# Row sums of exp(a) in a two-layer graph kernel: by a row of ones, or by partition

## The chip, the cores and the metric

The kernel runs on one core of a Trainium2 chip. Times are device microseconds of that core, and the metric is the median of several runs. Everything is in fp32; each fp32 matmul of the program appears in the profile as two TensorE instructions.

## The reference

The input is `x` (3327 x 512) and a sparse, symmetric-pattern adjacency `adj` (3327 x 3327). Two layers follow one another.

```
h = relu(layernorm(x))
a = (h Wq^T + bq)(h Wk^T + bk)^T / sqrt(512) + adj + adj
x = x + softmax(a, axis=-1) (h Wv^T + bv)

h = relu(layernorm(x))
A2 = adj + I
dscale = diagonal(A2) ** -0.5
x = x + relu((dscale[:,None] * A2 * dscale[None,:]) @ (A2 @ h @ W^T))
```

The softmax has a denominator for each row of `a`: the sum of exp(a) over 3327 entries. The change concerns these sums alone.

## The kernel before

Rows are padded to 3328, which is 26 tiles of 128. The kernel has three parts: it makes h^T and the queries, then the scores and their exponentials, then three large products (with exp(a), and twice with `adj`), each a one-level seven-multiplication scheme over 2 x 2 blocks.

**The scores.** The transposed scores are made in four groups, one for each entry (s, q) of `groups = [(1, 0), (0, 0), (0, 1), (1, 1)]`. Strip s has 2 x 7 tiles of 128 columns (s = 0) or 2 x 6 (s = 1); a group takes a half q of it, so its width `wd` is 448 columns (s = 0) or 384 (s = 1), for both halves y of the strip. Within a group the loop runs over 13 pairs of row tiles (`HALF = 13`). A step is one pair: `Pair.multiply` issues seven products of two program matmuls each (28 TensorE instructions) into banks of PSUM called X, Y and Z, and after each product VectorE adds it into the tile `g` (lines 557 and 565). ScalarE takes the exponentials (560 and 567). The work of neighbouring steps is put between the products by a hand-written list of seven entries, `beside_of(k)`, whose entry runs after a given product. In this loop VectorE, TensorE, GpSimd and SyncE keep the order of the program (`in_order`); ScalarE does not, and at the border to the next stage, which has an order of its own, the build interleaves the two.

**What accumulates.** The rows of a step lie on the partitions, so summing over rows of the transposed scores means summing over partitions and over the 13 steps. `Pair.gather` adds, step by step, two combinations of the exponentials into the tile `acc` (128 x 2 x wd): `acc[:, 0]` holds the sum of S1 terms and `acc[:, 1]` that of S4 terms, as the seven-multiplication scheme has made them. The sums of the strip's second half are those of `acc[:, 0]`; those of its first half are `acc[:, 1]` minus `acc[:, 0]`. It runs at two steps' distance: the last pair of a group is gathered in the second step of the next group.

**What turns it into sums.** `Pair.total(m)`, lines 601 to 613, runs once per group and m, two entries apart in the same step. It multiplies a column of ones (the stationary operand, 128 x 1) with `acc[:, m]` (the moving one, 384 or 448 columns), so that one row of sums lands on partition 0 of PSUM. VectorE copies that row (609) or subtracts the earlier one from it (611), and SyncE stores it to `totd` in DRAM (613). The last group is dealt with in the second step of the graph stage by `totals()`, which gives both sums the same bank, `ROLE["p8"]`; the others take turns in banks 6 and 7 (`tp_bank`).

**What reads it.** Two steps later `load_totals` (674) loads `totd` back as `tot`, 128 x 26, so that the sum of a row stands on the partition of that row. `prepared` takes the reciprocal (740), `judge` (691 to 703) tests the range of the sums, and `attend` (1016) scales rows with the reciprocal, some 400 us later.

**The graph stage.** `Step.multiply` (912) takes the seven products of one step, 14 instructions of 384 or 448 columns; its left operands, tiles `part`, are loaded three steps ahead by SyncE and summed by VectorE (175 to 177), its right operands `b` are loaded as `rows` and `row` (852) and combined (182 to 185, 873). A list `between` gives the step in which each further task runs.

Elsewhere in the kernel, line 463 multiplies a stationary 128 x 128 tile with the column of ones, four times in a row, for the bias of the queries; and 305 is a warm-up of TensorE at the start on a tile `zero`, which VectorE fills after three smaller memsets.

Of the kernel before, what the change touches and what calls it, by code (L numbers as in the profile page):

```python
# [10 lines left out]
F32 = mybir.dt.float32  # L11
# [4 lines left out]
P = 128  # L16
# [19 lines left out]
HALF = 13  # L36
PAIRS = 6
STRIPS = (0, 14)
HT = (7, 6)
# [8 lines left out]
def graph_layers_kernel(  # L48
# [29 lines left out]
    nc = tc.nc  # L78
    N = out.shape[0]
    NP, D = x.shape  # L80
# [29 lines left out]
    def bank(k, name):  # L110
        return banks.tile([P, BW], F32, name=name, tag=f"bank{k}")
# [27 lines left out]
    const = ctx.enter_context(tc.tile_pool(name="const", bufs=1))  # L139
    dram = ctx.enter_context(tc.tile_pool(name="dram", bufs=1, space=bass.MemoryType.DRAM))  # L140
# [5 lines left out]
    nc.vector.memset(mhalf, -0.5)  # L146
    ones = const.tile([P, 1], F32, name="ones")
    nc.vector.memset(ones, 1.0)

    pad = const.tile([P, 1], F32, name="pad")  # L150
    nc.vector.memset(pad, 0.0)
# [6 lines left out]
    tot = const.tile([P, NT], F32, name="tot")  # L158
# [5 lines left out]
    qd = dram.tile([P, DC, NP], F32, name="qd")  # L164
    pd = [[dram.tile([P, len(E_AT), H[s]], F32, name=f"p{s}_{t}") for t in range(HALF)] for s in range(2)]
    sumd = [[dram.tile([P, len(SUMS), H[s]], F32, name=f"sum{s}_{t}") for t in range(HALF)] for s in range(2)]
    totd = dram.tile([1, NP], F32, name="totd")
    x1d = [dram.tile([P, D], F32, name=f"x1d{i}") for i in range(NT)]
    rowd = [[dram.tile([P, D], F32, name=f"row{g}_{i}") for i in range(NT)] for g in range(3)]
    normd = {k: [dram.tile([1, 2 * 4 * P], F32, name=f"norm{m}_{k}") for m in range(2)] for k in range(4)}  # L170
# [56 lines left out]
    def psum_ring(*ks):  # L227
        turn = itertools.cycle(ks)
        return lambda name: bank(next(turn), name)

    x_bank, y_bank, z_bank, tp_bank = psum_ring(0, 1), psum_ring(2, 3), psum_ring(4, 5), psum_ring(6, 7)
# [203 lines left out]
    ps = [bank(k, "mm") for k in range(DC)]  # L435
    begun = h_transposed(TURN[0], psum_ring(6, 7, 4, 5))
    weighed = half(12, [P, D], "weighed")
    for c in range(DC):
# [8 lines left out]
        for r in range(DC):  # L447
            nc.tensor.matmul(ps[r], w_q[c // 2][:, c % 2, r * P : (r + 1) * P], w_k[c // 2][:, c % 2],
                             start=c == 0, stop=c == DC - 1)
# [60 lines left out]
    def adjacency(s, q, t):  # L510
# [6 lines left out]
            nc.sync.dma_start(g[k], src[:, :, c : c + wd])  # L517
        return g

    class Pair:  # L520


# [68 lines left out]
        def gather(self, m):  # L591

            if self.t == 0 and m == 0:
                Pair.acc = acc_ring([P, 2, Q[0]], "acc")[:, :, : self.wd]
            acc, new = Pair.acc, self.last if m else self.g[0][:, 1]
            if self.t == 0:
                nc.scalar.copy(acc[:, m], new)
            else:
                nc.vector.tensor_add(acc[:, m], acc[:, m], new)

        def total(self, m, own=None):

            if self.t < HALF - 1:
                return
            acc, ps = Pair.acc, own or tp_bank("tot")
            nc.tensor.matmul(ps[:1, : self.wd], ones, acc[:, m], start=True, stop=True)
            row = acc[:1, m]
            if m == 0:
                nc.vector.tensor_copy(row, ps[:1, : self.wd])
            else:  # L610
                nc.vector.tensor_sub(row, ps[:1, : self.wd], acc[:1, 0])
            c0 = (STRIPS[self.s] + (1 - m) * HT[self.s]) * P + self.c
            nc.sync.dma_start(totd[:, c0 : c0 + self.wd], row)


    pairs = {}
# [7 lines left out]
    def beside_of(k):  # L624
        def on(j, what, *args):
            if 0 <= j < len(steps):
                getattr(pairs[j], what)(*args)

        def difference():
            if k < len(steps) and steps[k][1] >= 6:  # L630
                next(more_of, None)

        return (
            lambda: (on(k - 2, "s4"), on(k - 2, "gather", 0)),
            lambda: (on(k - 1, "s3"), on(k - 2, "gather", 1)),
            lambda: on(k + 1, "sum_of_adjacency", 0),
            lambda: on(k + 1, "sum_of_adjacency", 1),
            lambda: (on(k - 2, "total", 0), difference()),
            lambda: (on(k - 2, "total", 1), on(k - 1, "s1")),
            lambda: on(k - 1, "s2"),  # L640
        )

    coming = queries(0)
# [7 lines left out]
    with in_order(*(e.engine for e in (nc.vector, nc.tensor, nc.gpsimd, nc.sync))):  # L651
        for k, (n, t) in enumerate(steps):
            if t == 0:
                qt = coming
            fetch(k + 2)
            if t == 2 and n + 1 < len(groups):
                coming = queries(n + 1)
                more_of = more_queries(n + 1, coming)
            beside = beside_of(k)
            pairs[k].multiply(qt)  # L660
        k = len(steps)
        beside = beside_of(k)
        for what in beside[:2]:
            what()
        Chain.finish()
        for what in (*beside[5:], *beside_of(k + 1)[:2]):
            what()

    def totals():
        for m in range(2):  # L670
            pairs[len(steps_of_scores) - 1].total(m, bank(ROLE["p8"], "tot"))

    def load_totals():
        nc.sync.dma_start(tot, totd[0].rearrange("(i p) -> p i", p=P))

    steps_of_scores = steps

# [2 lines left out]
    ROLE = {"p1": 0, "p6": 2, "p7": 4, "p5": 6, "p2": 7, "p3": 1, "p4": 5, "p8": 3}  # L680
# [79 lines left out]
    def difference():  # L760
        next(differences[0])
# [359 lines left out]
    def number_of(g, r, s, t):  # L1121
        return ((g * len(ORDER) + r) * 2 + s) * len(every) + t

    def at(k, what, *args):
        between.setdefault(k, []).append((what, args))

    early = []
    for g in range(3):
        for n, r in enumerate(ORDER):
            for t, e in enumerate(every):  # L1130
                k = number_of(g, n, 0, t)
# [9 lines left out]
    for n, job in enumerate(jobs):  # L1141
        k = k0 + n * (k1 - k0) // len(jobs)
# [15 lines left out]
    k = number_of(0, 5, 1, 2)  # L1158
# [6 lines left out]
    k = number_of(1, 5, 1, 2)  # L1165
# [9 lines left out]
    for (n, s, t), its in {  # L1175
# [4 lines left out]
        for i, when in zip(its, (between, within)):  # L1180
            if i is not None:
                k = number_of(2, n, s, t)
# [3 lines left out]
        rows(2, number_of(2, 4, 0, t + 2), i, (1,))  # L1186
    for n, i in enumerate(range(20, NT, 2)):
        at(number_of(2, 6, 1, 2) + n, last_load, i)
    for k, what in ((1, totals), (3, load_totals), (2, prepare), (6, prepared), (8, judge), (9, judged)):
        at(k, what)  # L1190
    k = number_of(1, 4, 0, 0)
    at(k, other_weights)
# [480 lines left out]
```

## Time and profile before

| | us |
|---|---|
| median of 3 runs | 2176.13 |
| lowest and highest run | 2174.09, 2177.01 |
| span of the profiled execution, first to last instruction | 2173.6 |
| the profiled execution's own time beside its span | not listed; the runs lie 0.5 to 3.4 above the span |
| TensorE busy | 2155.3 (99%) |
| VectorE busy | 1671.8 (77%) |
| ScalarE busy | 236.3 (11%) |
| DMA queues, share of 16 engines | 70.5% and 8.7% |
| the 16 instructions of line 606 | 244.2 to 639.1 us from the start, 511 ns by the median |
| the 8 VectorE instructions of lines 609 and 611 | 245.1 to 639.6 us, 576 ns by the median |

In the profile PE is TensorE's matmul row and PEld its weight loads, which can run beside a matmul. DVE is VectorE, ACT ScalarE, POOL GpSimd and SP SyncE, which only issues DMAs here. A timeline row gives the start in us, the length in us, the engine, the line, the operation, what is written and read, the shape of the stationary operand (for TensorE) and of the data, and the count of instructions merged into it; in brackets stands the idle time ahead of it, and what ended that. Lengths of matmuls overlap, because an instruction's end includes a modelled tail; starts are the better measure of pace. The mean granted TensorE clock is 0.999 of full speed.

### The profile page before, as it was taken

How to read it: one execution, taken by the hardware profiler on the slowest of the kernel's cores; microseconds unless marked ns; L12 is line 12 of the kernel's file. 1: busy time of each engine (PE TensorE's matmuls, PEld its weight loads, DVE VectorE, ACT ScalarE, POOL GpSimd, SP SyncE). 2: the span in 40 equal slices, each digit the busy share in tenths (PEclk: the TensorE clock that was granted, in tenths of full speed). 3: DMA queues.
4: the chain of work that ended last, by engine and by line, in shares of the span. 5: the costliest groups of instructions: out<-in, count | busy, mean ns of one | idle time of the engine just before them, and what ended most of it. 6: DMA issues, size and time to landing. Idle time of an engine off the chain costs nothing.

```text
span 2173.6 us, 21026 instructions
## 1 busy us (share of the span) xinstructions
PE 2155.3 (99%) x6378; PEld 1189.6 (55%) x6378; DVE 1671.8 (77%) x3256; ACT 236.3 (11%) x359; POOL 50.8 (2%) x62
## 2 busy tenths in 40 slices
PE   9999999999999999999999999999999999999998
PEld 5555555455555555555454555555666655555555
DVE  7479888888877688877778777987676667778686
ACT  6312111112110000000001000000011100000011
POOL 2000000000000000000111000000000000000000
PEclk9999999999999999999999999999999999999999
DMA  8678888889989899889787889986646468766695
GB/s 303 208 257 300 302 302 277 303 283 312 310 282 316 293 371 327 278 295 309 265 311 260 303 285 357 313 307 212 215 136 204 142 199 276 254 190 211 217 304 194
DMA packets 302030, 586.04 MB, mean 270 GB/s; under 512 B 34626, under 2 KB 169684, under 8 KB 301908
## 3 DMA queue, kind: packets, MB, share of 16 engines
q1 hardware_dynamic: 266614, 515.12, 70.5%
q10 hardware_dynamic: 35294, 69.48, 8.7%
q8 instruction: 53, 0.87, 0.2%
q14 instruction: 69, 0.57, 0.1%
HBM read 416.64 MB, written 167.86 MB: 269 GB/s over the span
## 4 chain that ended last, share of the span: by engine, by line
PE 91%; DVE 4%; DMA 4%; issue 1%; SPq 0%; POOL 0%; ACT 0%; ACTq 0%; DVEq 0%
PE p L912 52%; PE Y L553 13%; PE Z L553 7%; PE p L904 5%; PE p L1004 4%; PE pw L1065 3%; PE X L553 3%; PE Y L409 2%; DMA rows<-row 1%; PE Z L409 1%; DMA xt<-in_x_dram 1%; DVE part L175 1%; DMA part<-sum 1%; PE pt L1094 1%; PE X L409 0%
## 5 line engine op out<-in xcount | busy, mean ns | idle before, releaser
L912 PE MATMUL p<-part,b 128*128 128x448 f32 (+1 forms) x3528 | 1261.7, 513 | 2.2 <-DVE part L176 1.3
L912 PEld LDWEIGHTS p<-part,b 128*128 128x128 f32 x3528 | 668.0, 190 | 537.0 <-issue 286.1
L553 PE MATMUL Y<-qt,hp 128*128 128x448 f32 (+1 forms) x832 | 308.4, 513 | 1.7 <-DVE g L565 1.7
L175 DVE TENSOR_TENSOR part<-part 128x896 f32<-128x896 f32 (+1 forms) x252 | 256.8, 1019 | 67.3 <-DMA part<-sum 29.1
L553 PEld LDWEIGHTS Y<-qt,hp 128*128 128x128 f32 x832 | 157.7, 190 | 136.0 <-issue 72.3
L553 PE MATMUL Z<-qt,hp 128*128 128x384 f32 (+1 forms) x416 | 162.6, 513 | 0.0
L177 DVE TENSOR_TENSOR part<-part,part 128x448 f32<-128x448 f32 (+1 forms) x219 | 129.4, 591 | 14.9
L176 DVE TENSOR_TENSOR part<-part,part 128x448 f32<-128x448 f32 (+1 forms) x219 | 129.4, 591 | 7.2
L904 PE MATMUL p<-part,b 128*128 128x448 f32 (+1 forms) x336 | 124.2, 513 | 0.0
L553 PEld LDWEIGHTS Z<-qt,hp 128*128 128x128 f32 x416 | 78.8, 190 | 67.4 <-issue 37.4
L557 DVE SCALAR_TENSOR_TENSOR g<-g,Y 128x384 f32<-128x384 f32 (+1 forms) x156 | 91.4, 586 | 31.4 <-PE Y L553 30.3
L904 PEld LDWEIGHTS p<-part,b 128*128 128x128 f32 x336 | 63.7, 190 | 53.5 <-issue 31.4
L940 ACT COPY part<-p 128x384 f32<-128x384 f32 (+1 forms) x33 | 16.6, 502 | 660.2 <-PE p L912 543.2
L553 PE MATMUL X<-qt,hp 128*128 128x384 f32 (+1 forms) x208 | 81.1, 513 | 0.0
L560 ACT ACTIVATE g<-g 128x768 f32<-128x768 f32 (+1 forms) x48 | 43.0, 896 | 348.4 <-DVE g L557 298.7
L1004 PE MATMUL p<-w,ct 128*128 128x512 f32 x136 | 61.8, 594 | 0.4 <-DVE part L1016 0.4
L941 DVE TENSOR_TENSOR part<-p,part 128x384 f32<-128x384 f32 (+1 forms) x33 | 19.3, 585 | 52.9 <-PE p L912 52.2
L553 PEld LDWEIGHTS X<-qt,hp 128*128 128x128 f32 x208 | 39.5, 190 | 33.1 <-issue 19.3
L1065 PE MATMUL pw<-w,rows 128*128 128x256 f32 x208 | 53.6, 380 | 0.8 <-DVE rows L1055 0.8
L995 DVE TENSOR_TENSOR job<-job 128x896 f32<-128x896 f32 (+1 forms) x52 | 52.9, 1017 | 0.0
L202 POOL TENSOR_TENSOR rstd<-ve,mhalf 128x1 f32<-128x1 f32 x46 | 38.0, 828 | 555.4 <-DVE ve L200 520.9
L565 DVE TENSOR_TENSOR g<-g,Z 128x384 f32<-128x384 f32 (+1 forms) x52 | 30.4, 585 | 26.5 <-PE Z L553 26.4
(196 smaller groups left out, 1692.9 us busy)
## 6 DMA issues: line engine op xcount, KB each, us to landing
part<-sum SPq DMA_DIRECT2D x104, 448.0 KB, 5.3
part<-p SPq DMA_DIRECT2D x91, 448.0 KB, 6.0
part<-sum SPq DMA_DIRECT2D x104, 384.0 KB, 3.5
part<-p SPq DMA_DIRECT2D x91, 384.0 KB, 4.7
part<-in_adjT_dram SPq DMA_DIRECT2D x78, 448.0 KB, 4.8
b<-row SPq DMA_DIRECT2D x234, 128.0 KB, 5.0
part<-in_adjT_dram SPq DMA_DIRECT2D x78, 384.0 KB, 3.7
g<-in_adjT_dram SPq DMA_DIRECT2D x52, 448.0 KB, 4.1
```

The lines of the kernel that those rows point to most:

```text
L175: yield nc.vector.tensor_add(o[:, 0:2], g[:, 0:4:3], g[:, 1:2].to_broadcast([P, 2, g.shape[-1]]))
L176: yield nc.vector.tensor_add(o[:, 2], o[:, 1], g[:, 0])
L177: yield nc.vector.tensor_add(o[:, 3], o[:, 2], g[:, 2])
L409: nc.tensor.matmul(ps[:, :w], M[B[name]][:, c, o * P : (o + 1) * P], hp[k][:, A[name], c], start=start and c == 0, stop=c == 1, skip_group ...
L553: nc.tensor.matmul(ps[:, :wd], h_of(self.t, name, k), qt[B[name]][:, k], start=start and k == 0, stop=k == 1, skip_group_check=True)
L557: nc.vector.scalar_tensor_tensor(a[n], a[n], 2.0, ps[:, :wd], op0=ALU.mult, op1=ALU.add if sign > 0 else ALU.subtract)
L560: nc.scalar.activation(g[1], g[1], AF.Exp, **({"bias": pad} if self.t == HALF - 1 else {}))
L904: yield nc.tensor.matmul(ps[("p2", "p3", "p4", "p8")[k]][:, :w], b[:, z], a[:, 0, y], start=k == 3, stop=True)
L912: yield nc.tensor.matmul(ps[r][:, :w], b[:, i], m, start=self.t == 0, stop=self.t == PAIRS - 1 and r in ("p1", "p5", "p6", "p7"))
L995: nc.vector.tensor_add(self.a, self.a, self.b)
L1004: nc.tensor.matmul(ps, cts[s][y][d][:, k * P : (k + 1) * P], w[d], start=d == 0, stop=d == DC - 1)
L1065: nc.tensor.matmul(ps, a, W[B[name]][:, c], start=new and c == 0, stop=c == 1, skip_group_check=True)
```

## The change

The stationary operand is now a block of 128 columns of `acc`, and the moving operand has one or two columns, so that the sums of 128 rows land on 128 partitions of PSUM. Block c takes two program matmuls: `acc[:, 0]` against the two columns of `signs` (-1 and 1) into columns c and c + 4 of a bank, then `acc[:, 1]` against `ones`, accumulated into column c. The subtraction is thus done within TensorE. A group of 448 columns takes four blocks (the fourth overlaps the third, since 448 is three and a half tiles), one of 384 takes three. They are spread over four entries of `beside_of`, one step later than before. `place` then copies the columns from PSUM into `tot` on ScalarE: one copy for a group of s = 1, two or three where half tiles have to change partitions. DRAM is no longer involved: `totd`, its stores and `load_totals` are gone.

```diff
+    signs = const.tile([P, 2], F32, name="signs")
+    nc.vector.memset(signs[:, 0:1], -1.0)
+    nc.vector.memset(signs[:, 1:2], 1.0)
...
-    totd = dram.tile([1, NP], F32, name="totd")
...
+    TOTALS = (4, 3)
...
             acc, new = Pair.acc, self.last if m else self.g[0][:, 1]
+            self.acc = acc
...
-        def total(self, m, own=None):
+        def total(self, c, own=None):
+
+            if self.t < HALF - 1 or c >= TOTALS[self.s]:
+                return
+            if c == 0:
+                Pair.ps = own or tp_bank("tot")
+            acc, ps = self.acc, Pair.ps
+            o = min(c * P, self.wd - P)
+            nc.tensor.matmul(ps[:, c : c + 5 : 4], acc[:, 0, o : o + P], signs, start=True, stop=False, skip_group_check=True)
+            nc.tensor.matmul(ps[:, c : c + 1], acc[:, 1, o : o + P], ones, start=False, stop=True, skip_group_check=True)
+
+        def place(self):
 
             if self.t < HALF - 1:
                 return
-            acc, ps = Pair.acc, own or tp_bank("tot")
-            nc.tensor.matmul(ps[:1, : self.wd], ones, acc[:, m], start=True, stop=True)
-            row = acc[:1, m]
-            if m == 0:
-                nc.vector.tensor_copy(row, ps[:1, : self.wd])
+            ps = Pair.ps[:, :8].rearrange("p (y c) -> p y c", y=2)
+            to = tot[:, STRIPS[self.s] : STRIPS[self.s] + 2 * HT[self.s]].rearrange("p (y c) -> p y c", y=2)
+            h = P // 2
+            if self.s == 1:
+                nc.scalar.copy(to[:, :, 3 * self.q : 3 * self.q + 3], ps[:, :, 0:3])
+            elif self.q == 0:
+                nc.scalar.copy(to[:, :, 0:3], ps[:, :, 0:3])
+                nc.scalar.copy(to[:h, :, 3:4], ps[h:, :, 3:4])
             else:
-                nc.vector.tensor_sub(row, ps[:1, : self.wd], acc[:1, 0])
-            c0 = (STRIPS[self.s] + (1 - m) * HT[self.s]) * P + self.c
-            nc.sync.dma_start(totd[:, c0 : c0 + self.wd], row)
+                nc.scalar.copy(to[h:, :, 3:6], ps[:h, :, 0:3])
+                nc.scalar.copy(to[:h, :, 4:6], ps[h:, :, 0:2])
+                nc.scalar.copy(to[:, :, 6:7], ps[:, :, 3:4])
...
-            lambda: on(k + 1, "sum_of_adjacency", 0),
-            lambda: on(k + 1, "sum_of_adjacency", 1),
-            lambda: (on(k - 2, "total", 0), difference()),
-            lambda: (on(k - 2, "total", 1), on(k - 1, "s1")),
-            lambda: on(k - 1, "s2"),
+            lambda: (on(k + 1, "sum_of_adjacency", 0), on(k - 3, "total", 0)),
+            lambda: (on(k + 1, "sum_of_adjacency", 1), on(k - 3, "total", 1)),
+            lambda: (on(k - 3, "total", 2), difference()),
+            lambda: (on(k - 3, "total", 3), on(k - 1, "s1")),
+            lambda: (on(k - 3, "place"), on(k - 1, "s2")),
...
     def totals():
-        for m in range(2):
-            pairs[len(steps_of_scores) - 1].total(m, bank(ROLE["p8"], "tot"))
-
-    def load_totals():
-        nc.sync.dma_start(tot, totd[0].rearrange("(i p) -> p i", p=P))
+        ps, last = bank(ROLE["p8"], "tot"), pairs[len(steps_of_scores) - 1]
+        for c in range(4):
+            last.total(c, ps)
+        last.place()
...
-    for k, what in ((1, totals), (3, load_totals), (2, prepare), (6, prepared), (8, judge), (9, judged)):
+    for k, what in ((1, totals), (2, prepare), (6, prepared), (8, judge), (9, judged)):
```

## The prediction

> **What bounds the kernel now.** I read the page's busy times and its chain first, then TensorE's timeline around the instructions that the change replaces, then the earlier row that looks like what replaces them. From the page:
>
> ```profile
> PE 2155.3 (99%) x6378; PEld 1189.6 (55%) x6378; DVE 1671.8 (77%) x3256; ACT 236.3 (11%) x359; POOL 50.8 (2%) x62
> PE 91%; DVE 4%; DMA 4%; issue 1%; SPq 0%; POOL 0%; ACT 0%; ACTq 0%; DVEq 0%
> ```
>
> TensorE is busy for 99% and makes up 91% of the chain that ended last; only 18.3 us of the span (2173.6 - 2155.3) are not matmul. So an edit is priced in TensorE time first. In the stage of the scores the two stretches that I looked at have no TensorE gap at all, and VectorE is at 80 to 90% (busy time in windows; the columns are length, then busy time and count of PE, PEld, DVE, ACT, POOL, the clock, the DMA share, GB/s):
>
> ```profile
> 98.90:236.20 137.30, 137.30 (x423) 80.18 (x422) 109.55 (x218) 26.86 (x35) 0.00 (x0) 1.00 0.78 267
> 520.00:610.00 90.00, 90.00 (x279) 52.22 (x278) 81.25 (x171) 17.66 (x22) 0.00 (x0) 1.00 0.93 318
> ```
>
> Now TensorE's timeline around the first pair of sums (start, length, operation; each fp32 matmul of the program is two instructions, so "x2" is one sum):
>
> ```profile
> 238.10 1.67 PE L553 MATMUL Z<-qt,hp 128*128 128x448 f32 x4
> 239.60 1.67 PE L553 MATMUL X<-qt,hp 128*128 128x448 f32 x4
> 241.11 3.17 PE L553 MATMUL Y<-qt,hp 128*128 128x448 f32 x8
> 244.21 0.81 PE L606 MATMUL tot<-acc,ones 128*1 128x384 f32 x2
> 244.94 1.77 PE L553 MATMUL Z<-qt,hp 128*128 128x448 f32 x4
> 246.64 0.81 PE L606 MATMUL tot<-acc,ones 128*1 128x384 f32 x2
> 247.38 3.27 PE L553 MATMUL Y<-qt,hp 128*128 128x448 f32 x8
> ```
>
> The starts give the true pitch; the lengths include a modelled tail. Four of 448 columns take 239.60 - 238.10 = 1.50 us, so 0.376 each. Y x8 from 241.11 should make room at 241.11 + 3.01 = 244.12; the sum starts at 244.21 (0.09 late), streams 2 x 0.323 (the pitch of 384 columns: 9.03 us for 28 in the chain at 663.82), the next product starts 0.09 after that, and its four take 1.77 instead of 1.67 (0.10 more). A sum of 384 columns therefore costs **0.93 us** on TensorE: 0.65 of streaming and 0.28 at its edges. One of 448 costs 0.65 + 0.107 + 0.28 = 1.04.
>
> The last pair lies in the first steps of the graph stage, and its second sum waits:
>
> ```profile
> 628.20 9.18 PE L912 MATMUL p<-part,b 128*128 128x448 f32 x24
> 637.32 0.81 PE L606 MATMUL tot<-acc,ones 128*1 128x384 f32 x2
> 638.76 0.81 PE L606 MATMUL tot<-acc,ones 128*1 128x384 f32 x2 [0.64 <-DVE acc L609]
> 639.50 2.90 PE L912 MATMUL p<-part,b 128*128 128x448 f32 x7
> ```
>
> Both sums use one bank, so the second waits for VectorE's copy of the first. From 628.20 + 24 x 0.376 = 637.22 to 639.50 + 0.10 this pair costs **2.38 us**.
>
> **What the Trainium skill says.** "TensorE: Matmul & The Clock Gate", section "LDWEIGHTS (loading the stationary operand)", puts a weight load at its columns / 1.2 ns, so 107 ns for 128 columns whatever the matmul behind it. The same page, "Step-by-step: what each phase is for", says that TensorE pulls a load ahead of a running matmul where nothing conflicts. This trace agrees on both: loads of 128 columns follow each other 0.11 us apart (row below), and between equal shapes no load is exposed. It also shows where this fails: at L606, 128x1 amid 128x128, edges appear on both sides. "DMA: Bandwidth & Descriptors", "Rules for kernel authors", says that a strided last dimension becomes one descriptor per element; the load of `tot` (26 x 128 elements of 4 bytes) is of that kind, and here it landed in 5.0 us.
>
> **The change, part by part.** *Removed from TensorE:* 8 sums: two of 384 columns (2 x 0.93), four of 448 (4 x 1.04), the last pair 2.38. That is 1.86 + 4.16 + 2.38 = **8.40 us**.
>
> *Added to TensorE:* per column block two program matmuls, so four instructions, each with a 128x128 load and one or two moving columns. Blocks per group are 3, 4, 4, 3, so 14 blocks and 56 instructions against 16. The nearest row is the bias vector at L463, the same shape with one moving column:
>
> ```profile
> 21.49 0.97 PEld L463 LDWEIGHTS pu<-ones,weighed 128*128 128x128 f32 x8
> 21.60 0.95 PE L463 MATMUL pu<-ones,weighed 128*128 128x1 f32 x8
> ```
>
> One load takes 190 ns by the page's row, so eight in 0.97 us are (0.97 - 0.19) / 7 = 0.111 us apart; and its matmul starts at 21.60, right on the 0.109 pitch of the 128x128 transposes ahead of it, with no edge. A block of four costs 4 x 0.111 = 0.45: the first load hides under the product before, the next three and that of the product after are exposed. 56 x 0.1116 (0.78 us over the seven intervals, unrounded) = **6.25 us**. A bound below is the skill's 107 ns: 5.99. A bound above is that each insertion (11 single blocks and the last group's three together) keeps the 0.28 of edges that L606 has: 6.25 + 12 x 0.28 = 9.61. I take 6.25, because L463 has the new shape and L606 the old one.
>
> *VectorE:* four copies and four subtractions of one row go, 8 x 0.576 = 4.6 us. Six of them lie in the scores, where VectorE already keeps ahead of TensorE; worth nothing there. The last two end the 0.64 us wait, counted above.
>
> *ScalarE:* seven copies out of PSUM of up to 128 x 2 x 3 elements. No such row; the smallest PSUM copies here are about 0.5 us for 384 columns, so 0 to 0.5 each, in an engine that is 11% busy; an added copy can't gain. If one is put ahead of an exp, that is late by at most this, and its readers come a step (10 us) later. Cost 0; +0.5 each, 3.5 in all, if that cover were gone.
>
> *SP and DMA:* eight stores of a row leave SP's queue, and the load of `tot`. SP stood 4.6 us for the last first-row store (SyncE's waits: `L613 <- DVE acc L609`); behind it queue the next `part` loads, the weights and the diagonal. They can go out some microseconds earlier, and 3,328 four-byte elements leave a stage with a DMA share of 0.9. But from 640 to 1041 us TensorE stands for nothing (window: busy 401.00 of 401.00 us). Gain 0, at most the odd tenth.
>
> *A step later:* a group's sums go from the second to the third step of the next group; accumulation was complete either way, so no new wait. *`tot`* is read first at 666.4 us; both ways lie ahead of that. *Two memsets* of 128x1 stand ahead of `zero`, which starts TensorE's warm-up; memsets start 0.03 us apart, so +0.06.
>
> Sum: -8.40 + 6.25 + 0.06 = **-2.1 us**, bounds -2.4 and +1.3. Against the profiled execution, 2173.6 - 2.1 = 2171.5. The page gives no time of it beyond the span; the median of the runs is 2.5 above, so 2174.0.
>
> **The rivals.**
> - *Edges stay* (the other side). A mode switch or a self-wait drains TensorE at every insertion. Place: twelve insertions in the score stage and at 637 us; price 9.61 - 8.40 + 0.06 = +1.3, so 2177.4. It decides once a block costs over 8.40 / 14 = 0.60 us. For it: every L606 has edges. Against: L463 has none ahead of it.
> - *The seam of the stages moves.* At 624.6 us TensorE stands 1.65 us (`L553 ... [1.65 <-DVE g L565]`), since a graph-stage subtraction that waited 2.80 us for `rows` was put ahead of the scores' last ones on VectorE. Across this seam the order isn't written by hand, so the build may choose another: without the stall 2174.0 - 1.8 = 2172.2, with as much again 2175.8.
> - *Data doesn't come earlier.* From 1280 to 1380 us the DMA share is 0.99 and TensorE stands 2.1 us for `part` and `rows`. If those transfers keep their own clock, TensorE arrives 2.1 us earlier and waits as much longer: 2176.1. Against: the loads go out when TensorE frees their buffers, so they move with it.
>
> **How the numbers follow.** The sum as it stands 0.55, edges 0.10, seam better 0.14, seam worse 0.06, gain lost to data 0.10, something unseen 0.05. The runs shown spread over 2.9 us, and 0.2% (4.35 us) is about what a measurement of this kernel can tell from no change. Faster by more means below 2171.8: a fifth of the first case, half of the better seam, a little of the rest: 0.20. Slower by more needs two of the bad cases or something unseen: 0.09. Within: 0.71. The range 2170.5 to 2178.0 holds the better seam with some spread and the edges.
>
> **What would show it.** Right: no L606 at 128*1; blocks of x4 at 128*128 with 0.45 us between the products around them and no longer product behind; the 0.64 us wait gone; TensorE busy down by some 2 us; VectorE down by 4.6. Wrong: products behind a block that are 0.1 longer and start 0.09 late (edges), a longer gap near 625 us (seam), longer gaps at 1325 and 1366 us (data). A move of over 5 us either way would mean that I missed a mechanism.

## The result, and the profile after

After the change the kernel takes 2170.49 us (2168.28 to 2173.21), measured beside 2173.98 us for the kernel before (2171.90 to 2177.01) on the same chip. The ratio is 0.9984 [0.9978, 0.9990], about 3.5 us less, with 2.2 to 4.8 inside the interval. That lies within the 0.2% that I counted as no change. A second measurement on another chip (experiment 1) gave 0.9982 [0.9976, 0.9989], which is 2.4 to 5.2 us less.

From the page after, busy time and the chain of waits:

```profile
PE 2155.0 (99%) x6418; PEld 1195.6 (55%) x6418; DVE 1667.4 (77%) x3250; ACT 237.2 (11%) x366; POOL 51.1 (2%) x62
PE 91%; DVE 4%; DMA 4%; issue 1%; POOL 0%; ACT 0%; ACTq 0%; SPq 0%; DVEq 0%
```

TensorE has 40 instructions more (56 - 16), and VectorE is 4.4 us lighter, for the predicted 4.6. The chain is unchanged. TensorE's busy time went down by only 0.3 us, though the span went from 2173.6 to 2170.9. A matmul's busy time runs to its modelled end, so 56 short instructions with tails of their own aren't comparable with 16 long ones. The starts have to be read.

TensorE's timeline around the first group's blocks, after (start, length, operation):

```profile
250.53 1.67 PE L557 MATMUL X<-qt,hp 128*128 128x448 f32 x4
252.03 0.28 PE L614 MATMUL tot<-signs,acc 128*128 128x2 f32 x2
252.17 0.36 PE L615 MATMUL tot<-ones,acc 128*128 128x1 f32 x2
252.39 1.75 PE L557 MATMUL Y<-qt,hp 128*128 128x448 f32 x4
253.98 0.28 PE L614 MATMUL tot<-signs,acc 128*128 128x2 f32 x2
254.12 0.36 PE L615 MATMUL tot<-ones,acc 128*128 128x1 f32 x2
254.34 1.75 PE L557 MATMUL Y<-qt,hp 128*128 128x448 f32 x4
```

Each block is four instructions at 128*128. From one Y to the next is 254.34 - 252.39 = 1.95 us; the four instructions of a Y take 1.50, so the block costs **0.446** (predicted 0.45). Its first instruction starts on the products' pitch (250.53 + 1.50 = 252.03): there is no edge ahead. The last group, after:

```profile
626.86 9.18 PE L930 MATMUL p<-part,b 128*128 128x448 f32 x24
635.88 0.28 PE L614 MATMUL tot<-signs,acc 128*128 128x2 f32 x2
...
636.91 0.36 PE L615 MATMUL tot<-ones,acc 128*128 128x1 f32 x2
637.13 5.13 PE L930 MATMUL p<-part,b 128*128 128x448 f32 x13
```

Its twelve instructions take 637.13 - 635.88 plus 0.08 behind them, 1.33 us, where the two sums before took 2.38. VectorE's copy and the 0.64 us wait for it are gone. With eleven blocks inside the scores, 11 x 0.446 + 1.33 = 6.24 us (predicted 6.25). TensorE's first instruction starts at 1.20 us instead of 1.14: the 0.06 of the two memsets.

Of the places that I named as possible surprises, the seam, the border between the scores and the graph stage, had moved. TensorE's timeline and VectorE's, before:

```profile
626.81 1.56 PE L553 MATMUL Y<-qt,hp 128*128 128x384 f32 x4 [1.65 <-DVE g L565]
624.47 0.69 DVE L873 TENSOR_TENSOR b<-rows 128x512 f32<-128x512 f32 x1 [2.80 <-DMA rows<-row]
```

TensorE's, after:

```profile
625.46 1.56 PE L557 MATMUL Y<-qt,hp 128*128 128x384 f32 x4 [1.20 <-DVE g L569]
```

And VectorE's:

```profile
623.12 0.69 DVE L891 TENSOR_TENSOR b<-rows 128x512 f32<-128x512 f32 x1 [2.35 <-DMA rows<-row]
623.73 0.55 DVE L569 TENSOR_TENSOR g<-g,Z 128x384 f32<-128x384 f32 x1
```

The same subtraction stands ahead of the same additions as before, and waits 2.35 us for its rows instead of 2.80; TensorE's gap, the idle time in brackets, is 1.20 instead of 1.65. Step by step the direct sum is thus confirmed at 6.24 + 0.06 - 8.40 = -2.1, and the measured gain is 1.4 us more: the sum lies at the edge of the first interval and outside the second. The experiments ask whether the parts of the sum are right in the total time too, and where the rest is from.

### The profile page after: what moved, and what is told of

Read it like the earlier page. It is cut to its first block, busy times and chain, and to the rows that moved or that the text cites. A ratio compares the mean times of both kernels' runs of the same rounds, so it can differ in the third digit from the quotient of the medians.

```text
span 2170.9 us, 21088 instructions
## 1 busy us (share of the span) xinstructions
PE 2155.0 (99%) x6418; PEld 1195.6 (55%) x6418; DVE 1667.4 (77%) x3250; ACT 237.2 (11%) x366; POOL 51.1 (2%) x62
## 2 busy tenths in 40 slices
DMA packets 298670, 586.01 MB, mean 270 GB/s; under 512 B 31274, under 2 KB 166324, under 8 KB 298548
## 4 chain that ended last, share of the span: by engine, by line
PE 91%; DVE 4%; DMA 4%; issue 1%; POOL 0%; ACT 0%; ACTq 0%; SPq 0%; DVEq 0%
PE p L930 52%; PE Y L557 13%; PE Z L557 7%; PE p L922 5%; PE p L1022 3%; PE pw L1083 3%; PE X L557 3%; PE Y L411 2%; PE Z L411 1%; DMA part<-sum 1%; DMA rows<-row 1%; DMA part<-p 1%; DVE part L177 1%; PE pt L1112 1%; PE X L411 0%
```

## The experiments

All were timed in five rounds beside the kernel before. Theory A: the direct sum of 2.1 and, for the rest, the seam. Theory B: the side work (VectorE's row operations, SyncE's stores, the strided load) costs time after all.

**1. The change once more**, unedited, as the reference for edits of it.

> The kernel after, unchanged, for what two profiles of one kernel differ by. Theory (TensorE time of the sums, -2.1, is all that is systematic): the block costs repeat to 0.01 us, while the start (0.4 us later than before in the first profile), the gap at the seam (1.20) and the waits for data between 757 and 785 us and at 1298, 1324 and 1366 us come out differently; the median is 2 us below before. Rival (another 1.4 us come from the side work that is gone, so the whole is -3.5): those waits repeat, and the median is again 3.5 below before.

Measured: 2170.36 us, ratio 0.9982 [0.9976, 0.9989]. The gain repeats; so it isn't a chance of one chip. In time it is the rival's 3.5 and not the theory's 2. The waits for data that the rival named did not repeat, though: this profile shows none at 784 or 1325 us, and a gap of 0.53 us at the seam.

**2. The kernel before without its sums.**

```diff
-            if self.t < HALF - 1:
-                return
+            return
...
-        nc.sync.dma_start(tot, totd[0].rearrange("(i p) -> p i", p=P))
+        nc.vector.memset(tot, 1.0)
```

> The kernel before without the sums at all (tot is filled with ones, so the softmax isn't normalized): no matmul of line 606, no VectorE row, no store, no strided load. Theory: the sums cost before their 8.40 us of TensorE, so the median falls by 8.4 (from 7.5 to 9.3). If data set the pace of the graph stage, so that TensorE time saved ahead of it is lost there again, it falls by clearly less, 5 or so. If the side work cost more than TensorE shows, by 10.

Measured: 2165.5 us, ratio 0.9962 [0.9948, 0.9976], so 8.4 us less, what removal of the eight sums was priced at; with five runs the interval is 5.2 to 11.3 us, so the agreement to the tenth is luck. On TensorE the products close up where L606 stood:

```profile
241.02 3.17 PE L553 MATMUL Y<-qt,hp 128*128 128x448 f32 x8
244.03 1.67 PE L553 MATMUL Z<-qt,hp 128*128 128x448 f32 x4
245.53 3.17 PE L553 MATMUL Y<-qt,hp 128*128 128x448 f32 x8
```

From 241.02 to 244.03 is eight times 0.376, and Z is back at 1.67. This kernel also lacks the side work of the sums; the interval is too wide to tell from it what that costs. In the profiled execution not all of the time comes back: from their first product to the graph stage's first the scores take 510.3 us instead of 514.6, 4.3 less where six sums are 6.0, and VectorE waits 2.78 us for `rows` at 513 us, a wait that experiment 8 comes back to.

**3. The change with every block issued twice.**

```diff
+            for _ in range(2):
-            nc.tensor.matmul(ps[:, c : c + 5 : 4], acc[:, 0, o : o + P], signs, ...)
-            nc.tensor.matmul(ps[:, c : c + 1], acc[:, 1, o : o + P], ones, ...)
+                nc.tensor.matmul(ps[:, c : c + 5 : 4], acc[:, 0, o : o + P], signs, ...)
+                nc.tensor.matmul(ps[:, c : c + 1], acc[:, 1, o : o + P], ones, ...)
```

> The kernel after with every column block issued twice (the second overwrites the first, same sums). Theory: 14 blocks more, the eleven single ones 0.446 each since the repeated block follows without an edge, and 12 instructions more in the last group: 56 x 0.1116 = 6.2 us above after, so some 4 us above before. If a block's time is hidden in part beside other work, less than 5 above after.

Measured: 2177.1 us, ratio 1.0015 [1.0008, 1.0021], 6.7 us over experiment 1; the second blocks were to cost 6.2. The price of a block holds in the total time, and in the trace of the scores, whose stretch is 4.9 us longer for eleven second blocks. In the profiled execution something was added, seen in the weight loads behind the last group's 24 instructions (engine PEld):

```profile
644.28 0.30 PEld L616 LDWEIGHTS tot<-ones,acc 128*128 128x128 f32 x2
644.51 0.38 PEld L931 LDWEIGHTS p<-part,b 128*128 128x128 f32 x2
645.29 0.33 PEld L931 LDWEIGHTS p<-part,b 128*128 128x128 f32 x1 [0.41 <-issue]
646.04 0.33 PEld L931 LDWEIGHTS p<-part,b 128*128 128x128 f32 x1 [0.41 <-issue]
646.79 0.33 PEld L931 LDWEIGHTS p<-part,b 128*128 128x128 f32 x1 [0.41 <-issue]
```

They follow each other 0.75 us apart instead of 0.376, and the granted clock was 0.50 from 646 to 648 us. The 56 instructions of 448 columns that follow took 22.82 us up to the next product (644.54 to 667.36), 1.8 more than 56 x 0.376. I return to that below.

**4. The kernel before with a stationary operand of 128x128 ones**, so that the sums have the shape of the products around them.

```diff
+    wide = const.tile([P, P], F32, name="wide")
+    nc.gpsimd.memset(wide, 1.0)
...
-            nc.tensor.matmul(ps[:1, : self.wd], ones, acc[:, m], start=True, stop=True)
+            nc.tensor.matmul(ps[:, : self.wd], wide, acc[:, m], start=True, stop=True)
```

> The kernel before with the stationary column of ones widened to 128 x 128, all else as before (the row is read from partition 0). Theory (the edges of 0.28 us at each sum come from the change of the stationary shape between 128 and 1 columns): the edges vanish, a sum of 384 columns costs 0.65 and one of 448 0.75, in all 8 x 0.28 = 2.2 us less, the wait of 0.64 in the last pair stays; median some 2 us below before. Rival (the edges belong to a wait of this line on a semaphore, or to the accumulator being read): they stay, and the time stays.

Measured: 2172.03 us, ratio 0.9990 [0.9984, 0.9997], 1.9 us less (expected 2.2). TensorE's timeline:

```profile
241.35 3.17 PE L555 MATMUL Y<-qt,hp 128*128 128x448 f32 x8
244.36 0.81 PE L608 MATMUL tot<-acc,wide 128*128 128x384 f32 x2
245.00 1.67 PE L555 MATMUL Z<-qt,hp 128*128 128x448 f32 x4
```

The sum starts at 241.35 + 3.01 = 244.36, with no 0.09 ahead of it; 0.64 later Z starts, and its four take 1.67, not 1.77. All of the 0.28 us at the edges of a sum is gone. So the edges belong to the change of the stationary operand's width, 128 to 1 and back (with which the output goes from 128 partitions to one; the edit changes both), and not to having a short foreign matmul between the products, nor to the semaphores and the accumulator, which are the same. It fits that the new blocks, 128 wide, have none. The wait of the last pair stays:

```profile
626.83 1.68 PE L555 MATMUL Y<-qt,hp 128*128 128x384 f32 x4 [2.90 <-DVE g L567]
628.30 10.80 PE L914 MATMUL p<-part,b 128*128 128x448 f32 x24
638.93 0.81 PE L608 MATMUL tot<-acc,wide 128*128 128x384 f32 x2
640.38 0.91 PE L608 MATMUL tot<-acc,wide 128*128 128x384 f32 x2 [0.64 <-DVE acc L611]
```

In this execution the seam's gap was 2.90 us and the 24 instructions behind it took 10.80 instead of 9.18: a bad draw in the one execution that is profiled, beside which the median still shows most of the expected gain.

**5. The change with the side work of the old way put back**: two row operations on VectorE and two stores for each group, and the strided load, all of it unused.

```diff
+            for m in range(2):
+                row = self.acc[:1, m]
+                nc.vector.tensor_scalar(row, row, 1.0, None, op0=ALU.mult)
+                c0 = (STRIPS[self.s] + (1 - m) * HT[self.s]) * P + self.c
+                nc.sync.dma_start(totd[:, c0 : c0 + self.wd], row)
...
+    def load_totals():
+        nc.sync.dma_start(idle_tot, totd[0].rearrange("(i p) -> p i", p=P))
```

> The kernel after with the side work of before put back: per group two VectorE instructions on a row of acc behind the last block, two stores of that row to DRAM by SyncE, and the strided load of 3,328 elements in the fourth step of the graph stage, into a tile that nobody reads. TensorE's instructions are those of after, in the same order. Theory A (side work is hidden; what the medians show beyond the 2.1 us comes from the gap at the seam): the time stays at that of after within half a microsecond, or moves with the gap at the seam alone. Theory B (the side work costs 1.4 us, through later loads): 1.4 above after, and the waits for data near 760 to 785 or 1298 to 1366 us are longer.

Measured: 2170.64 us, ratio 0.9987 [0.9980, 0.9994]: 0.3 us over experiment 1 by the medians and 1.1 by the ratios, whose intervals overlap. Theory B wanted 1.4, which the times alone don't exclude. The spans speak against it: from the first to the last instruction the median run takes 2168.5 us here and 2168.6 in experiment 1, and in its profile TensorE waits only 0.43 us for data between 757 and 1366 us. So eight row operations, eight stores and the load of 3,328 single elements are hidden within the span, as the prediction had them. What is longer is the rest of a run's time, outside its span: 2.14 us by the mean, against 1.81 in experiment 1 and 2.09 in the kernel before. The side work seems to cost some 0.3 us there; which part of it does, isn't shown (experiment 9, with stores and load, has 1.88).

**6 and 7. The seam taken out of both kernels.** The subtraction of the seam is held behind the scores' last addition, in the change (6) and in the kernel before (7):

```diff
-                nc.vector.tensor_add(a[n], a[n], ps[:, :wd])
+                Pair.end = nc.vector.tensor_add(a[n], a[n], ps[:, :wd])
...
-                yield nc.vector.tensor_sub(own, self.two[:, :, 0:E], self.two[:, :, E:D])
+                ins = nc.vector.tensor_sub(own, self.two[:, :, 0:E], self.two[:, :, E:D])
+                if self.g == 0 and self.its[0] == 3:
+                    after(ins, Pair.end)
+                yield ins
```

> The kernel after with one dependency more: the first VectorE instruction of the graph stage's right operand for t = 3 (it waits 1.7 to 2.3 us for its rows) is held behind the last addition of the scores. Theory A (TensorE's gap of 0.5 to 2.9 us at 625 us comes from that instruction standing ahead of the scores' last additions, and a gap of over 2 us brings some 1.5 us of slow clock behind it): the gap goes, to below 0.4 us, there are no slow matmuls behind it, and the median is 0.6 to 1.2 below after. Rival (the rows are needed soon after anyway, so the gap only moves by some steps): the same time as after.

> The kernel before with the same dependency. Theory A (beyond the 2.1 us of TensorE time, after gains by a shorter seam): without the seam on both sides the difference of the two kernels shrinks to the 2.1 us, so this is 2.1 above the kernel after with the dependency, and 1.5 to 2.6 below before. Theory B (side work): the difference stays 3.5, so this is about 1 below before and 3.5 above its partner.

Measured: 2170.12 us (0.9980 [0.9973, 0.9987]) and 2173.29 us (0.9992 [0.9983, 1.0000]). TensorE at the seam in experiment 6:

```profile
622.94 0.92 PE L933 MATMUL p<-part,b 128*128 128x448 f32 x2
623.75 1.56 PE L557 MATMUL Y<-qt,hp 128*128 128x384 f32 x4
625.14 5.05 PE L933 MATMUL p<-part,b 128*128 128x448 f32 x13
```

The gap is gone, yet the median falls by only 0.2 us against experiment 1, and the two kernels without the seam's gap are still 3.2 us apart by their medians, 2.6 by their ratios. If the seam were the source of the excess, they would be 2.1 apart; Theory A also wanted 0.6 to 1.2 of gain in 6 and 1.5 to 2.6 in 7, where 0.8 was measured. The intervals are too wide to exclude it (some 1.5 us on each ratio), but Theory A gets no support. The numbers are nearer to Theory B's, about 1 and 3.5, whose side work experiment 5 doesn't confirm; neither theory fits all three.

**8. The kernel before once more**, profiled again.

> The kernel before, unchanged: its second profile, and what a comparison of a kernel with itself gives. Expected: ratio 1 within 0.0007; the costs of the eight sums repeat (0.93, 1.04 and 2.38 us), the gap at the seam, the start and the waits for data come out differently. Theory A expects a gap at the seam of 1.6 us or more, and if it is over 2 us, slow matmuls behind it; theory B expects a gap as in after, 0.5 to 1.2 us, and longer waits for data between 757 and 1366 us.

Measured: 2174.72 us, ratio 1.0000 [0.9991, 1.0008]; span 2171.6. The last pair of sums costs 2.37 us again. TensorE's timeline at the seam:

```profile
624.85 1.67 PE L912 MATMUL p<-part,b 128*128 128x448 f32 x4
626.64 1.56 PE L553 MATMUL Y<-qt,hp 128*128 128x384 f32 x4
```

VectorE's timeline some 110 us earlier, in the same execution:

```profile
516.97 0.69 DVE L873 TENSOR_TENSOR b<-rows 128x512 f32<-128x512 f32 x1 [1.87 <-DMA rows<-row]
517.58 0.55 DVE L557 SCALAR_TENSOR_TENSOR g<-g,Y 128x384 f32<-128x384 f32 x1
```

In this execution the seam costs the kernel before next to nothing: 626.64 - 624.85 is 1.79 with 1.50 of products in it, where Theory A asked for 1.6 or more of gap, and Theory B for 0.5 to 1.2 and longer waits behind it. The gap follows the arrival of one transfer, which differs from execution to execution. Without the seam's edit it is 1.65, 0.12, 1.09 and 2.90 us in four profiles with the old way's order (before, 8, 2 and 4), and 1.20, 0.53, 0.13 and 2.13 in four with the new (after, 1, 5 and 3): too scattered to tell the versions apart. The expectations' threshold of 2 us for slow matmuls behind a gap isn't borne out either: experiment 3 had 2.13 and none directly behind it.

What does recur is the wait at 513 to 518 us, an early subtraction of the graph stage that waits for rows ahead of the scores' additions. It left a TensorE gap of 0.34 us here. After, it is short:

```profile
514.12 0.69 DVE L891 TENSOR_TENSOR b<-rows 128x512 f32<-128x512 f32 x1 [0.38 <-DMA rows<-row]
```

VectorE waits 0.88 to 2.78 us at this place in all six profiles with the old order (before, 2, 4, 7, 8 and 9) and 0.32 to 0.60 in all five with the new (after, 1, 3, 5 and 6), so this wait does differ with the version. Experiment 2 has none of the side work and the longest wait, experiment 5 has it back and the shortest; so the side work isn't the cause, which stays open.

With several profiles of each kind, the span can be cut at the same products: at the first of the scores (108.90 us in the kernel before), at the first of the graph stage (623.49), and behind the last group's sums (639.60, 0.10 after the next product's start; 0.08 with the new blocks). Means of the kernels with the old sums (before, 7 and 8) and with the new blocks (after, 1, 5 and 6):

| Stretch | old sums | new blocks | difference |
|---|---|---|---|
| scores, up to the graph stage's first product | 514.67 us (514.41 to 515.01) | 513.30 us (all four) | -1.37 |
| last group's sums | 2.38 | 1.33 | -1.05 |
| from there to the end | 1533.4 (1532.2 to 1534.0) | 1532.6 (1531.9 to 1533.7) | -0.8 |

Of the first row, six sums less eleven blocks are 1.86 + 4.16 - 4.91 = 1.11; the other 0.26 is the wait at 513 to 518 us, which reaches TensorE in two of the three old kernels and in none of the four new. The last row is within the scatter of either kind; in it TensorE waits for data near 785, 1326 and 1367 us, 0.76 to 2.08 us in all in the three old and 0 to 0.80 in the four new. The seam's gap, cut out of the table, averages 0.59 us in these three old and 0.47 in the four new, where experiments 6 and 7 have none.

**9. The kernel before, improved without the change**: wide ones, the last group's second sum a step later, so that it needn't wait for the copy, and the seam's edit. The first and the last are the edits of 4 and 7; the other is this:

```diff
-        for m in range(2):
-            pairs[len(steps_of_scores) - 1].total(m, bank(ROLE["p8"], "tot"))
+        pairs[len(steps_of_scores) - 1].total(0, bank(ROLE["p8"], "tot"))
+
+    def totals_1():
+        pairs[len(steps_of_scores) - 1].total(1, bank(ROLE["p8"], "tot"))
...
-    for k, what in ((1, totals), (3, load_totals), ...
+    for k, what in ((1, totals), (2, totals_1), (3, load_totals), ...
```

> The kernel before, sums still as rows through DRAM, with its three losses taken out one by one: the ones widened to 128 x 128 (no edges), the last group's second sum one step later (no wait of 0.64 us for the copy of the first), and the dependency at the seam of r6 and r7. Theory (all that mattered was TensorE time; the way of the sums through DRAM is hidden): the eight sums cost only their streaming, 4 x 0.65 + 4 x 0.75 = 5.6 us, 2.8 less than before and 0.6 less than the blocks of after; the median is that of r6 or a little below, 2169 to 2170.5. Rival (avoiding DRAM and VectorE is worth a microsecond of its own): 1 to 1.5 above r6, 2171 to 2172.

Measured: 2171.12 us, ratio 0.9988 [0.9981, 0.9995], above the 2169 to 2170.5 that I expected, though only by 0.6 us, and within the rival's 2171 to 2172. Each sum does cost 0.65 us, as meant. The trace shows a new wait, which goes through three engines. SyncE's own instructions in its timeline:

```profile
641.78 0.24 SPq L615 DMA_DIRECT2D totd<-acc  x1
642.07 1.75 SPq L727 DMA_DIRECT2D w<-in_wvT_dram  x4
```

VectorE's timeline of the same kernel:

```profile
656.56 0.96 DVE L177 TENSOR_TENSOR part<-part 128x768 f32<-128x768 f32 x1 [12.15 <-DMA part<-p]
```

And TensorE's:

```profile
659.80 9.48 PE L919 MATMUL p<-part,b 128*128 128x384 f32 x28
670.72 0.21 PE L705 MATMUL p<-good,ones 128*1 128x26 f32 x2 [1.44 <-DVE most L702]
```

The later sum makes the last row's store later (641.78), and the weights, the diagonal and the next `part` queue behind it on SyncE. VectorE then waits 12.15 us for `part`, reaches the tests on `tot` late, and TensorE stands 1.44 us for the result. In experiment 7, with both sums together, the weights went out at 639.93, 2.1 us earlier, while TensorE came to this place (the x28) 2.3 us later; VectorE waited 9.49 us for the same `part`, and TensorE didn't feel it. The rival asks for 1 to 1.5 us, and this one wait is as much; so what the trace shows is a late store, not a fixed price of the way through DRAM.

## Why the prediction was right

*The main term was right in kind and in size.* The sums removed: 8.40 predicted, 8.4 (5.2 to 11.3) in the time of experiment 2. The blocks added: 6.25 predicted, 6.24 from the trace, and 6.7 in the time of experiment 3. Experiments 1 and 2, with the blocks and without any sums, lie only 4.9 us apart; that fits the longer wait for rows in the profile of 2, but isn't settled by five runs. The choice of L463 over L606 as the nearest row decided this, and experiment 4 shows why it was the right one: L606's edges come with its width of one column. "Edges stay" (+1.3) is refuted by the blocks' starts, and by the sign of the result. The bound below, the load at the skill's 107 ns ("TensorE: Matmul & The Clock Gate", section "LDWEIGHTS (loading the stationary operand)"), would have given 5.99; the measured 0.446 / 4 = 0.1115 is a little more. It is the pitch that agrees with the page; the record of a single load is 190 ns long.

*Where the gain comes from.* Of the 8.40, streaming is only 4 x 0.65 + 4 x 0.75 = 5.6. The blocks cost 6.24, more than that. The swap of the operands alone would thus lose 0.6; the gain on TensorE is the edges and the wait in the last pair, 2.8 together, and experiment 4 gets the edges' part without the swap.

*One sign was loosely put.* I wrote that right would be "no longer product behind", and the product behind is 0.08 us longer (1.75). I read that as the exposed load of its first instruction, which the 0.446 already holds, not an edge.

*The covers held, but for some 0.3 us.* VectorE's and SyncE's share was put at nothing: experiment 5 finds none within the span, and 0.3 outside it. That the strided load goes out as single elements is borne out: without it and the stores the page counts 31,274 packets under 512 bytes instead of 34,626. ScalarE's copies were bounded at 0.5 us each; they take 0.16. At 396.88 and 531.50 us an exp starts right behind them and may be some tenths late, which TensorE, busy for all of the windows around them, doesn't feel (rows of the tile `tot`):

```profile
L625 ACT COPY tot<-tot x2: 165/165/165, 256.5 to 637.3; 128x6 f32<-128x6 f32 x2
L628 ACT COPY tot<-tot x1: 158/158/158, 396.7 to 396.7; 64x2 f32<-64x2 f32 x1
```

SyncE's queue did come free earlier: VectorE takes the `part` of 657.29 us now at 647.91, and waits there for TensorE (its timeline, after).

```profile
647.91 0.96 DVE L177 TENSOR_TENSOR part<-part 128x768 f32<-128x768 f32 x1 [4.67 <-PE p L930]
```

It bought no time, since TensorE sets the pace there in both kernels; experiment 9 shows what can happen without it.

*The excess is not settled.* Of the 3.5 us between the forecast of 2174.0 and the measured 2170.49, 2.1 are the base: the three runs shown had a median of 2176.13, the nineteen beside the change 2173.98. The median therefore stands at the very edge of the stated range; on the base of the three runs the ratio makes it 2172.6, well inside. The other 1.4 is outside the sum. It also comes close to what "The seam moves" offered (2172.2, a gain of 3.9), but that is luck: the seam gives about 0.1 in the three and four profiles of the table and 0.4 over all those without its edit (the gap lies at 625.2 to 626.8 us there, not at 624.6).

The record shows where the rest lies, not why. In the table it is 0.26 in the wait near 515 us, which differs with the version, and 0.8 in waits for data from 785 us on, which may be chance; 0.28 more lies outside the span, where a run of the kernel before takes 2.09 us and one of the change 1.81. Together with the seam that is 1.5. "Data doesn't come earlier" didn't come true: TensorE's gain of the first 640 us survives to the end. With intervals from 2.2 and from 2.4 us it is unlikely that there is nothing beyond the sum of 2.1; a profile of many executions of each would tell.

Experiment 6, the change with the seam's edit, is the fastest with all of its work (2170.12), but not distinguishably faster than the change alone.

## What to carry to other kernels

Price an operation on a full TensorE by the pitch of starts on the nearest row with the same stationary shape; lengths and busy sums hide the difference (here 0.3 of busy time against 2.2 of pitch). Swapping the operands isn't a gain in itself: count the streamed columns that go (here 5.6 us) against the loads that come (6.24). A stationary operand as wide as its neighbours' spares the edges even without the swap. A gap that one transfer's arrival sets needs several profiles before any of it is credited to an edit.

## What the runs showed of the hardware that I had not expected

**The width of the stationary operand has a price of its own.** Going from 128x128 to 128x1 and back cost 0.09 us ahead, 0.09 behind and 0.10 in the next product, 0.28 a sum; with 128x128 ones (and 128 output partitions) it cost none, at the same streaming (experiment 4).

**A few matmuls at half the clock, after a short quiet stretch.** After the gap of 2.90 us in experiment 4 four instructions ran at half pace and a fifth in part (+1.6 us: 10.80 - 9.18). In experiment 3 a gap of 2.13 us did nothing at once, the 24 instructions behind it took the usual 9.18; but the 2.6 us of 24 instructions with one or two moving columns each (641.94 to 644.54) were followed by nearly five at half pace. Windows of experiment 4 and of experiment 3 (third column from the right: the clock):

```profile
625.00:632.00 7.00, 5.17 (x10) 2.73 (x11) 7.00 (x17) 1.78 (x2) 0.00 (x0) 0.76 0.46 164
646.00:648.00 2.00, 2.00 (x4) 1.00 (x3) 0.00 (x0) 0.00 (x0) 0.00 (x0) 0.50 1.22 118
```

Half that many short instructions, in the change itself, were not followed by it; windows of the change:

```profile
636.00:640.00 4.00, 4.00 (x21) 2.70 (x20) 2.77 (x7) 0.17 (x1) 0.00 (x0) 1.00 1.03 387
640.00:644.00 4.00, 4.00 (x13) 1.96 (x12) 2.68 (x4) 0.00 (x0) 0.00 (x0) 1.00 1.02 172
```

The clock stays at 1.00. The Trainium skill ("TensorE: Matmul & The Clock Gate", section "What's actually happening") puts the drop to half clock after an idle window of about 3.4 us that runs freely. Here less went ahead of it: 2.90 us of gap, and a stretch in which TensorE was busy by the profile. Each was seen in one execution. That the few moving columns are what counted as idle is my reading, not shown; the earlier gap of 2.13 us, 13 us ahead, isn't ruled out. It is a reason not to put many such blocks in one place.
